# Moving the sums of adj's rows into layer 1, with three buffers for the logits and one for the rows

## The chip, the cores and the metric

The kernel runs on one core of a Trainium2 chip. The metric is the device time of one execution in microseconds (us): the median of the runs. Engines are called by the names of the profile: PE is TensorE, PEld its weight loads, DVE is VectorE, ACT is ScalarE, POOL is GpSimd, SP is SyncE. A "line" such as L551 is a line of the kernel that the profile belongs to; from layer 1 on, the changed kernel's line numbers are 3 to 8 higher than those of the kernel before (ahead of it one lower), and the experiments' are one or a few higher still.

## The reference

Four layers over a graph of N = 2708 nodes with 256 features. `adj` is a dense 2708 x 2708 matrix of non-negative weights, about 29 MB. Each layer is followed by a residual and a layernorm.

```python
x = layernorm(x + adj @ x * W0)                     # layer 0
x = layernorm(x + gat4(x, adj > 0, W1, a1))         # layer 1: four heads of attention, then layernorm
# layer 2, "edge" and "node" parts
dn  = diag(adj);  A = adj - diag(dn)
edge = gru(A @ x, x, edge_weights)
node = gru(mean over 3 heads of (softmax(logits where A != 0) * A) @ x @ Wk, x, node_weights)
x = layernorm(x + dn * edge + dn * node)
# layer 3
deg = adj.sum(axis=1) + 1
x = layernorm(x + concat(x, (adj @ (x @ Wn.T)) / deg) @ Wl.T)
```

Three things are needed of adj's rows: the diagonal, the places that are zero (`none`), and the sum of each row for layer 3 (`deg`). Layer 2 also needs, for each row and each of the three heads, the maximum of the logits and the sum of their exponentials; they are called the row statistics here. Names that the profile lines use: `z` holds the logits of one head for 128 rows, `arow` a tile of adj's rows, `tr` the transposes that TensorE makes of x, `xt` their copy by ScalarE (TensorE's next matmuls read it), `supt` ScalarE's copy of s, `sr` the transposed row statistics, `whh` and `wih` the weights of the gated unit. PSUM is the memory that TensorE accumulates in.

## The kernel before

The 22 row tiles of 128 rows are grouped in six spans (five of 512 columns, one of 148). The edge stage makes, for each span, `s = adj_t-block @ x` on TensorE, and the row statistics of its tiles on VectorE and ScalarE; the gated unit ("unit") of a span is emitted after the statistics of the next.

```python
early = [turn[:, i * CB * W : (i + 1) * CB * W]... for i in range(2)]   # two blocks in an idle buffer
...
def row_stats(t):                                   # edge stage
    a = load_rows(nc.gpsimd, rows, t, 2)            # two buffers for adj's rows
    z = rows.tile([P, N], F32, tag="z", bufs=2)
    nc.scalar.activation(z[:n], a[:n], AF.Identity, accum_out=degree[:n])   # the sum; z is not used
    nc.vector.tensor_scalar(degree[:n], degree[:n], 1.0, None, ALU.add)
    nc.vector.reciprocal(rdeg[:n, t : t + 1], degree[:n])
    ...                                             # diagonal
    nc.vector.tensor_scalar(none[:n], a[:n], 0.0, NEG_INF, ALU.is_equal, ALU.mult)
    for k in range(K):                              # K = 3 heads
        if k: z = rows.tile([P, N], F32, tag="z", bufs=2)
        nc.vector.tensor_tensor_reduce(out=z[:n], in0=e_b[:n, k, :], in1=none[:n], ..., accum_out=st[...])
        nc.scalar.activation(z[:n], z[:n], AF.Exp, scale=-1.0, bias=st[...], accum_out=den[:n])
        nc.vector.reciprocal(st[:n, t, 1, k : k + 1], den[:n])

for g, (lo, hi) in enumerate(spans):                # edge stage
    ...                                             # 22 x 2 matmuls s <- block, x
    for f in range(FC): nc.scalar.copy(supt[:, f, :w], acc[f][:, :w])
    for t in range(lo, hi): row_stats(t)
    if g == len(spans) - 1: store_stats(ps_e, rows, *spans[0])
    if last: edge(*last)                            # unit of the span before: 4 transposes, xt copies, 24 matmuls
    last = (g, supt)
edge(*last)
```

In layer 1, four heads are accumulated for each span, and each result is copied from PSUM by ScalarE (`sum`). The rest of layer 1 (normalisation with a power on GpSimd, transposes on TensorE, copies `xt` on ScalarE) follows a span later.

The softmax here doesn't subtract the row's maximum and nothing guards it: scores larger than these inputs give would overflow.

Of the kernel before, what the change touches and what calls it, by code (L numbers as in the profile page):

```python
# [8 lines left out]
F32 = mybir.dt.float32  # L9
# [4 lines left out]
AF = mybir.ActivationFunctionType  # L14
ALU = mybir.AluOpType
# [3 lines left out]
P = 128  # L19
# [7 lines left out]
def kernel(  # L27
# [37 lines left out]
    def sz(i):  # L65
        return min(P, N - i * P)
# [11 lines left out]
    def pool(name, bufs=1, **kw):  # L78
# [16 lines left out]

    turn = xpool.tile([P, NT * F], F32, name="turn")
    x0 = h3 = [turn[:, t * F : (t + 1) * F] for t in range(NT)]
    early = [
        turn[:, i * CB * W : (i + 1) * CB * W].rearrange("p (c w) -> p c w", w=W)
        for i in range(NT * F // (CB * W))  # L100
    ]

    fall_d = dram.tile([H, N], F32, name="fall_d")
    e_d = dram.tile([K, N], F32, name="e_d")
# [4 lines left out]
    u_parts = xpool.tile([P, NT, 3, K], BF16, name="u_parts")  # L109

    rdeg = xpool.tile([P, NT], F32, name="rdeg")
    diag = xpool.tile([P, NT], F32, name="diag")

    st = xpool.tile([P, NT, 2, K], F32, name="st")
# [38 lines left out]
    def load_rows(queue, pool, t, bufs):  # L153
        a = pool.tile([P, N], F32, tag="arow", name="arow", bufs=bufs)
        queue.dma_start(a[: sz(t)], adj[t * P : t * P + sz(t), :])
        return a
# [18 lines left out]
    def weights(pool, name, w):  # L175
        wt = pool.tile([P, w.shape[0] // P, w.shape[1]], F32, name=name)
        nc.sync.dma_start(wt, w.rearrange("(c p) j -> p c j", p=P))
        return wt
# [33 lines left out]
    with pool("l1keep") as keep:  # L212
# [56 lines left out]
        with (  # L269
# [63 lines left out]
            with pool("l1", 2) as l1:  # L333

                def layer1_rest(t, o):
                    n = sz(t)
                    layernorm(o, o, n)
                    nc.vector.tensor_tensor(o[:n], o[:n], gamma_b[:n], ALU.mult)
                    nc.vector.tensor_tensor(o[:n], o[:n], beta_b[:n], ALU.add)
                    nc.vector.tensor_tensor(o[:n], o[:n], xs[t][:n], ALU.add)  # L340
                    layernorm(xs[t], o, n)

                    xt = transposed(ps_t, l1, xs[t], n, "xt")
                    pm = ps_m.tile([P, 2 * F], F32, tag="pm", name="pm")
                    for f in range(FC):
                        nc.tensor.matmul(
                            pm[:n, :K], xt[:, f, :n], uw[:, f, :], start=(f == 0), stop=(f == FC - 1)
                        )
                    left = pm[:n, :K]
                    for i in range(3):  # L350
                        nc.vector.tensor_copy(u_parts[:n, t, i, :], left)
                        if i < 2:
                            r = small.tile([P, K], F32, tag="u_left", name="u_left")
                            nc.vector.tensor_tensor(r[:n], left, u_parts[:n, t, i, :], ALU.subtract)
                            left = r[:n]

                def layer1_end(lo, hi, sums):

                    for t in range(lo, hi):
                        n = sz(t)  # L360
                        at = (t - lo) * P
                        pt = ps_t.tile([P, 4, P], F32, tag="tr", name="tr")
                        for h in range(H):
                            nc.tensor.transpose(
                                pt[:n, h, : HD + 1], sums[h][: HD + 1, at : at + n], ident[: HD + 1, : HD + 1]
                            )
                        rden = small.tile([P, H], F32, tag="rdenh", name="rdenh")
                        nc.vector.reciprocal(rden[:n], pt[:n, :H, HD])
                        o = l1.tile([P, F], F32, tag="o", name="o")
                        nc.vector.tensor_tensor(  # L370
                            o[:n].rearrange("p (h d) -> p h d", d=HD),
                            pt[:n, :H, :HD],
                            rden[:n, :, None].to_broadcast([n, H, HD]),
                            ALU.mult,
                        )
                        layer1_rest(t, o)



                done = None  # L380
                for lo, hi in spans:
                    at, w = lo * P, width(lo, hi)
                    sums = []
                    for h in range(H):
                        acc = ps_acc.tile([P, 512], F32, tag="acc", name="acc")
                        for c in range(NT):
                            k = sz(c)
                            p = l1.tile([P, W], F32, tag="p", name="p", bufs=6)
                            nc.vector.scalar_tensor_tensor(  # L389
                                p[:k, :w], fall_b[:k, h, at : at + w], rise[:k, c, h : h + 1],  # L390
                                mask[:k, c, at : at + w], ALU.max, ALU.mult,
                            )
                            nc.tensor.matmul(  # L393
                                acc[: HD + 1, :w], hs[c][:k, h, :], p[:k, :w], start=(c == 0), stop=(c == NT - 1)
                            )
                        sb = l1.tile([HD + 1, W], F32, tag=f"sum{h}", name=f"sum{h}", bufs=1 + (h == 0))
                        nc.scalar.copy(sb[:, :w], acc[: HD + 1, :w])  # L397
                        sums.append(sb)
                        if h == 0 and done:
                            layer1_end(*done)  # L400

                    for t in range(lo, hi):
                        n = sz(t)
                        own = mask[:n, t, t * P : t * P + n]
                        nc.gpsimd.tensor_tensor(own, own, offdiag[:n, :n], ALU.mult, saturate=False)
                    done = (lo, hi, sums)
                layer1_end(*done)
# [106 lines left out]
    with (  # L514
# [3 lines left out]
        pool("ps_e", 2, space=PSUM) as ps_e,  # L518
        pool("ps_g", 4, space=PSUM) as ps_g,
    ):  # L520
        wih, whh = weights(ework, "wih", e_wih), weights(ework, "whh", e_whh)
        b = gru_columns(ework, e_bih, e_bhh)
        e_b = rows.tile([P, K, N], F32, name="e_b")
# [3 lines left out]

        def row_stats(t):
            n = sz(t)
            a = load_rows(nc.gpsimd, rows, t, 2)  # L530
            z = rows.tile([P, N], F32, tag="z", name="z", bufs=2)
            degree = small.tile([P, 1], F32, tag="degree", name="degree")
            nc.scalar.activation(z[:n], a[:n], AF.Identity, accum_out=degree[:n])  # L533
            nc.vector.tensor_scalar(degree[:n], degree[:n], 1.0, None, ALU.add)
            nc.vector.reciprocal(rdeg[:n, t : t + 1], degree[:n])
            blk = a[:n, t * P : t * P + n]
            dtmp = rows.tile([P, P], F32, tag="dtmp", name="dtmp")
            nc.vector.scalar_tensor_tensor(
                dtmp[:n, :n], blk, 1.0, ident[:n, :n], ALU.mult, ALU.mult, accum_out=diag[:n, t : t + 1]
            )  # L540
            nc.vector.tensor_tensor(blk, blk, offdiag[:n, :n], ALU.mult)
            none = rows.tile([P, N], BF16, tag="none", name="none", bufs=2)
            nc.vector.tensor_scalar(none[:n], a[:n], 0.0, NEG_INF, ALU.is_equal, ALU.mult)
            for k in range(K):
                if k:
                    z = rows.tile([P, N], F32, tag="z", name="z", bufs=2)

                nc.vector.tensor_tensor_reduce(  # L548
                    out=z[:n], in0=e_b[:n, k, :], in1=none[:n], scale=-1.0, scalar=HIGHEST,
                    op0=ALU.add, op1=ALU.min, accum_out=st[:n, t, 0, k : k + 1],  # L550
                )  # L551
                den = small.tile([P, 1], F32, tag="den", name="den")
                nc.scalar.activation(  # L553
                    z[:n], z[:n], AF.Exp, scale=-1.0, bias=st[:n, t, 0, k : k + 1], accum_out=den[:n]
                )
                nc.vector.reciprocal(st[:n, t, 1, k : k + 1], den[:n])
# [11 lines left out]
        for g, (lo, hi) in enumerate(spans):  # L568
            w = width(lo, hi)
            acc = [ps_s.tile([P, W], F32, tag=f"s{f}", name=f"s{f}") for f in range(FC)]  # L570
            for bi, (c0, c1) in enumerate(blocks):
                if loads % 5 < len(early):
                    s = load_block(early[loads % 5], lo, hi, bi, None)
                else:
                    s = load_block(ework, lo, hi, bi, 5 - len(early))
                loads += 1
                for c in range(c0, c1):
                    k = sz(c)
                    for f in range(FC):
                        nc.tensor.matmul(  # L580
                            acc[f][:, :w], xs[c][:k, f * P : (f + 1) * P], s[:k, c - c0, :w],
                            start=(c == 0), stop=(c == NT - 1),
                        )
# [365 lines left out]
```

## Time and profile before

| | us |
|---|---|
| Time, median of the runs (2274.83 to 2279.68) | 2276.75 |
| Layer 1, first matmul to the first matmul of the u sums | 457.6 |
| Edge stage, its first matmul to the node stage's first | 379.2 |
| of which: first pass to last exponential (statistics) | 329.3 |
| of which: last exponential to the node stage (tail) | 38.0 |
| Node stage and layer 3 | 1084.4 |

Two more answers on the whole edge stage are wanted for the comparison. The first is its row of the stretches' busy times (columns: stretch, its length, then busy us and number of instructions of PE, PEld, DVE, ACT, POOL; granted clock, DMA share, GB/s). The second is the list of what TensorE waited for there (total us, times, longest).

```profile
809.80:1189.00 379.20, 334.09 (x886) 156.72 (x886) 286.65 (x422) 267.37 (x267) 18.76 (x32) 0.94 0.57 174
```

```profile
PE tr L464 <- ACT xt L465: 24.1, 8, 15.5
PE tr L464 <- ACT sr L478: 8.6, 2, 6.7
PE s L580 <- DMA blk<-in_adj_t_dram: 3.2, 1, 3.2
...
PE gate L437 <- ACT xt L465: 2.5, 1, 2.5
```

TensorE, not VectorE, is the busiest engine of the stage: 334 of 379 us. It idles 379.2 - 334.1 = 45.1 us, and 24.1 + 2.5 = 26.6 us of this are waits for the xt copies that stand in ScalarE's queue.

### The profile page before, as it was taken

What the parts mean: (1) busy time and instruction counts of PE and PEld (TensorE: products, weight loads), DVE (VectorE), ACT (ScalarE), POOL (GpSimd) and SP (SyncE); (2) the same over time, 40 slices, a digit from 0 to 9 for tenths busy, and PEclk for the clock granted to TensorE, in tenths of its full rate; (3) what the DMA queues carried; (4) which work ended last, traced back from release to release, by engine and by line L of the source; (5) the groups of instructions that cost most, each with busy time, mean ns of one, the idle gap of its engine ahead of it and who ended that gap; (6) DMA issues with size and microseconds to landing.
All of it is one profiled execution on the core that took longest, in us unless ns stands there. A gap on an engine that the chain in (4) does not pass through costs nothing.

```text
span 2273.4 us, 19055 instructions
## 1 busy us (share of the span) xinstructions
PE 2141.9 (94%) x6729; PEld 1094.7 (48%) x6729; DVE 1404.6 (62%) x2747; ACT 601.9 (26%) x937; POOL 175.8 (8%) x258
## 2 busy tenths in 40 slices
PE   5999999999999899999669999999999999979998
PEld 4777733333334334444434444444444444658886
DVE  4555578999988547888846656646646646441111
ACT  0000000000000147877743333333333323320000
POOL 0111100101101110000000000000000000011111
PEclk9999999999999799999879999999999999989999
DMA  5343320000000187654153300301212000014443
GB/s 185 134 146 136 138 54 0 0 0 0 1 0 1 64 253 240 206 183 154 50 159 108 100 30 19 102 28 38 83 38 65 21 22 24 1 70 149 171 165 120
DMA packets 163910, 196.57 MB, mean 86 GB/s; under 512 B 17218, under 2 KB 145511, under 8 KB 155464
## 3 DMA queue, kind: packets, MB, share of 16 engines
q1 hardware_dynamic: 154204, 147.74, 20.8%
q0 software_dynamic: 9600, 47.51, 6.0%
q8 instruction: 55, 0.90, 0.2%
q14 instruction: 51, 0.42, 0.1%
HBM read 186.75 MB, written 8.46 MB: 86 GB/s over the span
## 4 chain that ended last, share of the span: by engine, by line
PE 72%; DVE 16%; ACT 3%; issue 3%; POOL 3%; DMA 2%; SPq 1%; POOLq 0%; ACTq 0%; DVEq 0%
PE acc L670 25%; PE acc L173 16%; PE acc L393 11%; PE gate L437 7%; DVE p L389 5%; PE s L580 4%; DVE z L548 3%; POOL bn_rs L128 2%; PE gate L629 2%; PE pz L187 2%; ACT z L553 1%; ACT z L533 1%; DVE bn_st L122 1%; PE u L493 1%; PE tr L135 1%
## 5 line engine op out<-in xcount | busy, mean ns | idle before, releaser
L670 PE MATMUL acc<-p,x 128*128 128x512 f32 (+2 forms) x1584 | 620.7, 546 | 2.0 <-DVE p L668 2.0
L173 PE MATMUL acc<-turn,strip 128*128 128x256 f32 (+2 forms) x1936 | 444.9, 385 | 0.5 <-ACT lwn L266 0.5
L393 PE MATMUL acc<-p,h 128*65 128x512 f32 (+3 forms) x1056 | 425.6, 552 | 6.5 <-DVE p L389 5.5
L670 PEld LDWEIGHTS acc<-p,x 128*128 128x128 f32 (+1 forms) x1584 | 280.7, 191 | 308.5 <-issue 263.0
L173 PEld LDWEIGHTS acc<-turn,strip 128*128 128x128 f32 (+2 forms) x1936 | 350.1, 186 | 86.5 <-issue 35.0
L389 DVE SCALAR_TENSOR_TENSOR p<-fall_b,rise,mask 128x512 f32<-128x512 f32 (+2 forms) x528 | 354.1, 682 | 25.6 <-PE acc L393 6.9
L668 DVE TENSOR_TENSOR p<-p,blk 128x512 f32<-128x512 f32 (+2 forms) x396 | 245.7, 626 | 193.4 <-ACT p L667 192.1
L667 ACT ACTIVATE p<-p 128x512 f32<-128x512 f32 (+2 forms) x396 | 225.7, 578 | 380.3 <-DVE p L664 378.5
L393 PEld LDWEIGHTS acc<-p,h 128*65 128x65 f32 (+1 forms) x1056 | 137.0, 140 | 262.7 <-issue 137.2
L548 DVE CUSTOM_DVE_ANT_0 z<-e_b,none 128x2708 f32<-128x2708 f32 (+1 forms) x66 | 195.3, 2966 | 6.2 <-DMA e_b<-e_d 5.7
L553 ACT ACTIVATE z<-z,st 128x2708 f32<-128x2708 f32 (+1 forms) x66 | 168.2, 2549 | 74.0 <-DVE st L548 74.0
L664 DVE TENSOR_SCALAR p<-st_b,e_col 128x512 f32<-128x512 f32 (+2 forms) x396 | 175.2, 447 | 11.6 <-PE acc L670 11.2
L128 POOL TENSOR_TENSOR bn_rs<-bn_ve,neg_half 128x1 f32<-128x1 f32 (+1 forms) x110 | 74.5, 677 | 1107.8 <-DVE bn_ve L126 1104.3
L137 ACT COPY xt<-tr 128x256 f32<-128x256 f32 x66 | 24.0, 364 | 473.1 <-PE tr L135 464.4
L580 PE MATMUL s<-blk,x 128*128 128x512 f32 (+2 forms) x312 | 124.9, 555 | 3.2 <-DMA blk<-in_adj_t_dram 3.2
L437 PE MATMUL gate<-xt,whh 128*128 128x512 f32 (+1 forms) x288 | 123.6, 552 | 4.2 <-ACT xt L465 2.8
L697 DVE SCALAR_TENSOR_TENSOR o<-acc,rdeg,o 128x256 f32<-128x256 f32 (+1 forms) x22 | 10.6, 483 | 164.9 <-PE acc L173 164.9
L580 PE MATMUL s<-turn,x 128*128 128x512 f32 (+3 forms) x216 | 86.7, 551 | 2.8 <-ACT supt L586 2.8
L580 PEld LDWEIGHTS s<-blk,x 128*128 128x128 f32 (+1 forms) x312 | 56.8, 193 | 67.4 <-issue 66.7
L437 PEld LDWEIGHTS gate<-xt,whh 128*128 128x128 f32 x288 | 53.1, 195 | 62.8 <-issue 51.7
L397 ACT COPY sum<-acc 65x512 f32<-65x512 f32 (+1 forms) x24 | 12.6, 531 | 228.8 <-PE acc L393 228.8
L449 DVE SCALAR_TENSOR_TENSOR g_r<-g_r,g_h 128x512 f32<-128x512 f32 (+1 forms) x24 | 15.0, 625 | 86.7 <-ACT g_h L442 86.7
(133 smaller groups left out, 1435.3 us busy)
## 6 DMA issues: line engine op xcount, KB each, us to landing
strip<-in_adj_t_dram SPq DMA_DIRECT2D x44, 1408.0 KB, 6.1
blk<-in_adj_t_dram SPq DMA_DIRECT2D x168, 256.0 KB, 4.7
arow<-in_adj_dram POOLq DMA_DIRECT2D x21, 1354.0 KB, 6.5
turn<-in_adj_t_dram SPq DMA_DIRECT2D x42, 256.0 KB, 5.3
st_b<-st_d SPq DMA_DIRECT2D x5, 1536.0 KB, 6.3
fall_b<-fall_d POOLq DMA_DIRECT2D x5, 1024.0 KB, 6.5
blk<-in_adj_t_dram SPq DMA_DIRECT2D x33, 128.0 KB, 2.7
e_b<-e_d POOLq DMA_DIRECT2D x5, 768.0 KB, 5.2
```

The source lines that it names most:

```text
L128: nc.gpsimd.tensor_tensor(rstd[:n], ve[:n], neg_half[:n], ALU.pow)
L173: nc.tensor.matmul(acc, s[:k, c, :n], rhs(c)[:k], start=(c == 0), stop=(c == NT - 1))
L389: nc.vector.scalar_tensor_tensor(p[:k, :w], fall_b[:k, h, at : at + w], rise[:k, c, h : h + 1], mask[:k, c, at : at + w], ALU.max, ALU.mult,)
L393: nc.tensor.matmul(acc[: HD + 1, :w], hs[c][:k, h, :], p[:k, :w], start=(c == 0), stop=(c == NT - 1))
L437: nc.tensor.matmul(g[:, :w], lt, rt, start=(q == 0), stop=(q == len(terms) - 1))
L548: nc.vector.tensor_tensor_reduce(out=z[:n], in0=e_b[:n, k, :], in1=none[:n], scale=-1.0, scalar=HIGHEST, op0=ALU.add, op1=ALU.min, accum_o ...
L553: nc.scalar.activation(z[:n], z[:n], AF.Exp, scale=-1.0, bias=st[:n, t, 0, k : k + 1], accum_out=den[:n])
L580: nc.tensor.matmul(acc[f][:, :w], xs[c][:k, f * P : (f + 1) * P], s[:k, c - c0, :w], start=(c == 0), stop=(c == NT - 1),)
L664: nc.vector.tensor_scalar(p[:q, :w], st_b[:q, k, :w], e_col[:q, c, k : k + 1], 0.0, ALU.add, ALU.min)
L667: nc.scalar.activation(p[:q, :w], p[:q, :w], AF.Exp)
L668: nc.vector.tensor_tensor(p[:q, :w], p[:q, :w], blks[bi][:q, c - c0, :w], ALU.mult)
L670: nc.tensor.matmul(acc[f][:, :w], xs[c][:q, f * P : (f + 1) * P], p[:q, :w], start=(c == 0), stop=(c == NT - 1),)
```

## The change

Its intent: the sum of a row (2.54 us on ScalarE for each of 22 tiles) is taken out of the edge stage, where ScalarE and VectorE wait for each other, into layer 1, where ScalarE is empty. adj's rows have to be read twice for it. The sum no longer takes a z buffer, a third z buffer is added, and the row buffer and one early block pay for the memory.

```diff
-    early = [turn[:, i * CB * W : ...] for i in range(...)]      # two blocks
+    early = turn[:, : CB * W]...                                 # one block
+    row = turn[:, CB * W : CB * W + N]
+    nc.gpsimd.memset(rdeg, 1.0)
 ... in layer 1
+    def row_degree(t):
+        nc.sync.dma_start(row[:n], adj[t * P : t * P + n, :])
+        degree = small.tile([P, 1], F32, tag="degree", name="degree")
+        nc.scalar.activation(row[:n], row[:n], AF.Identity, accum_out=degree[:n])
+        nc.gpsimd.tensor_scalar(rdeg[:n, t : t + 1], degree[:n], 1.0, None, ALU.add)
 ...
                         sums.append(sb)
                         if h == 0 and done:
                             layer1_end(*done)
+                        if lo + h < hi:
+                            row_degree(lo + h)
 ... in the edge stage
+    nc.vector.reciprocal(rdeg, rdeg)
 ...
-            a = load_rows(nc.gpsimd, rows, t, 2)
-            z = rows.tile([P, N], F32, tag="z", name="z", bufs=2)
-            degree = small.tile([P, 1], F32, tag="degree", name="degree")
-            nc.scalar.activation(z[:n], a[:n], AF.Identity, accum_out=degree[:n])
-            nc.vector.tensor_scalar(degree[:n], degree[:n], 1.0, None, ALU.add)
-            nc.vector.reciprocal(rdeg[:n, t : t + 1], degree[:n])
+            a = load_rows(nc.gpsimd, rows, t, 1)
 ...
-                if k:
-                    z = rows.tile([P, N], F32, tag="z", name="z", bufs=2)
+                z = rows.tile([P, N], F32, tag="z", name="z", bufs=3)
 ...
-                if loads % 5 < len(early): s = load_block(early[loads % 5], ...)
-                else:                      s = load_block(ework, ..., 5 - len(early))
+                if loads % 5 == 0: s = load_block(early, ...)
+                else:              s = load_block(ework, ..., 4)
```

More of the change, by code (lines that the diff above doesn't have):

```diff
@@ L97 @@
     x0 = h3 = [turn[:, t * F : (t + 1) * F] for t in range(NT)]
-    early = [
-        turn[:, i * CB * W : (i + 1) * CB * W].rearrange("p (c w) -> p c w", w=W)
-        for i in range(NT * F // (CB * W))
-    ]
+    early = turn[:, : CB * W].rearrange("p (c w) -> p c w", w=W)
+    row = turn[:, CB * W : CB * W + N]
     fall_d = dram.tile([H, N], F32, name="fall_d")
@@ L376, in layer1_end @@
                         layer1_rest(t, o)
+                def row_degree(t):
+                    n = sz(t)
+                    nc.sync.dma_start(row[:n], adj[t * P : t * P + n, :])
+                    degree = small.tile([P, 1], F32, tag="degree", name="degree")
+                    nc.scalar.activation(row[:n], row[:n], AF.Identity, accum_out=degree[:n])
+                    nc.gpsimd.tensor_scalar(rdeg[:n, t : t + 1], degree[:n], 1.0, None, ALU.add)
                 done = None
@@ L571 @@
             for bi, (c0, c1) in enumerate(blocks):
-                if loads % 5 < len(early):
-                    s = load_block(early[loads % 5], lo, hi, bi, None)
+                if loads % 5 == 0:
+                    s = load_block(early, lo, hi, bi, None)
                 else:
-                    s = load_block(ework, lo, hi, bi, 5 - len(early))
+                    s = load_block(ework, lo, hi, bi, 4)
                 loads += 1
```

## The prediction

> **What bounds the kernel now.** The busy time of each engine in six stretches comes first, because the share over the whole span mixes stages with different limits.
>
> ```profile
> core 0: us, PE busy (x) PEld busy (x) DVE busy (x) ACT busy (x) POOL busy (x), PEclk, DMA share, GB/s
> ...
> 304.00:761.00 457.00, 440.12 (x1259) 157.25 (x1259) 409.19 (x887) 19.40 (x44) 51.11 (x63) 0.99 0.01 1
> ...
> 831.60:1150.00 318.40, 291.71 (x744) 134.33 (x745) 264.03 (x372) 249.47 (x235) 14.10 (x24) 0.95 0.55 170
> 1150.00:1189.00 39.00, 25.51 (x98) 15.26 (x96) 13.69 (x32) 13.06 (x28) 2.25 (x4) 0.81 0.62 178
> 1189.00:2030.00 841.00, 828.36 (x2222) 385.25 (x2222) 486.82 (x1028) 282.91 (x515) 25.87 (x43) 1.00 0.17 52
> ```
>
> The reader is to see: layer 1 (304 to 761 us) is bound by TensorE and leaves ScalarE empty (19 of 457 us) and the DMA too (1 GB/s). The edge stage (810 to 1189 us, where the row statistics run) has VectorE at 264 and ScalarE at 249 of 318 us, and in its last 39 us nothing is full. The node stage after it is full of TensorE; the change doesn't touch it, nor layer 3.
>
> Then VectorE's groups in 821 to 1151 us, for what each tile of statistics waits for:
>
> ```profile
> L548 DVE CUSTOM_DVE_ANT_0 z<-e_b,none 128x2708 f32<-128x2708 f32 x63 | 186.5, 2967 | 6.1 <-DMA e_b<-e_d 5.7
> L543 DVE TENSOR_SCALAR none<-arow 128x2708 bf16<-128x2708 f32 x20 | 31.4, 1570 | 0.0
> L556 DVE RECIPROCAL st<-den 128x1 f32<-128x1 f32 x63 | 9.9, 157 | 17.6 <-ACT z L553 17.5
> ...
> L534 DVE TENSOR_SCALAR degree<-degree 128x1 f32<-128x1 f32 x20 | 3.0, 152 | 26.9 <-ACT z L533 26.8
> ```
>
> So VectorE stands still 26.9 us for the sums of adj's rows and 17.6 us for reciprocals behind ScalarE. In time order, one tile shows how the sum does it:
>
> ```profile
> 980.26 0.29 DVE L538 SCALAR_TENSOR_TENSOR dtmp<-arow,ident 128x128 f32<-128x128 f32 x1
> ...
> 983.11 0.16 DVE L556 RECIPROCAL st<-den 128x1 f32<-128x1 f32 x1 [2.48 <-ACT z L553]
> 985.56 0.15 DVE L534 TENSOR_SCALAR degree<-degree 128x1 f32<-128x1 f32 x1 [2.28 <-ACT z L533]
> ```
>
> The sum also takes one of the two z buffers for its unused output, so ScalarE can't start it early. Last, TensorE's timeline at the end of the stage:
>
> ```profile
> 1117.54 1.98 PE L437 MATMUL gate<-supt,wih 128*128 128x512 f32 x4
> 1134.99 0.69 PE L464 MATMUL tr<-ident,x 128*128 128x128 f32 x2 [15.47 <-ACT xt L465]
> 1140.23 1.12 PE L464 MATMUL tr<-ident,x 128*128 128x128 f32 x4 [4.55 <-ACT xt L465]
> 1141.38 3.11 PE L437 MATMUL gate<-xt,whh 128*128 128x512 f32 x4
> ```
>
> TensorE had finished its span matmuls and idled 20 us, because the little copies of xt stand in ScalarE's queue behind exps. The statistics end at 1151 us, gates run to 1174, and the node stage's first matmul is at 1189.
>
> **What the Trainium skill says.** "TensorE: Matmul & The Clock Gate", section on the array as 16 32×32 sub-arrays: ScalarE's and VectorE's queues are strict FIFO. The trace agrees: xt's copy at 1134.59 us came only after the exp of 1132.04. "ScalarE: Activation LUTs", Rules for kernel authors: about 0.3 us + 0.83 ns per element, for 2708 elements 2.55 us; the trace has 2.46 us plus an accumulator read of 0.19, overlapping to 2.54. "DMA: Bandwidth & Descriptors", Anatomy of one DMA: 2.0 us + bytes/436e3, for a 1354 KB row tile 5.2 us; the trace has a median of 6.5 (arow) and 6.1 (a strip of 1408 KB), which I use. "Perfetto Trace Analysis", Optimization Strategy: the same gap repeating can mean too few buffers; the gap of 2.28 us repeats in most tiles.
>
> **The change, part by part.**
>
> *1. Removed from the edge stage.* 22 sums on ScalarE of 2.54 us (56 us), 22 adds and 22 reciprocals of 0.15 us on VectorE, which cost 0.2 us a tile (4 us), and the wait of 26.9 us. With a third z buffer most of the 17.6 us should go too. VectorE's floor, from the spacing in the trace: 66 passes at 2.96 us = 196; 20 masks (none; two fall before) at 1.6 = 32; 19 diagonals at 0.45 = 8.5; three gated units' arithmetic, 30 x 0.62 = 18.6; diagonal blocks 4.5. Sum 260 us. I add 20 us for stalls that I expect to stay: 5 for blocks from DMA (4.8 now), 5 for ScalarE's small work in between, 5 for row loads, 5 for matching with TensorE. TensorE has its own floor of the same size: counting 0.858 us a matmul from its timeline, it ends span 4 near 1071 us, where VectorE without stalls gets at 1075. So 282 us with the last exp, against 329 now (822 to 1151).
>
> *2. One buffer for adj's rows.* A load can start when none has been read (0.55 us later in the trace) and takes 6.5 us, so 7 us; VectorE has three passes, 8.9 us, meanwhile. Hidden, unless a load is slow (the slowest took 9.8 us). In the start of the stage it costs a little: row tile 1 is now asked for after two e_b broadcasts and stands in VectorE's order between small copies on which TensorE's transposes wait. I put 2.5 us.
>
> *3. One early block, four in the other pool.* Five buffers as before. TensorE has one block (8 matmuls, 6.9 us) instead of two before it waits for loads, but does 5 gate matmuls there that come later otherwise. Zero net.
>
> *4. Added to layer 1.* 22 loads, sums and GpSimd adds. One buffer makes them a serial chain: 2.54 us sum + 0.2 to the issue + about 6 us for the load = 8.7 us each, an estimate from the durations above. The first load queues behind a 1 MB block, so I count from 302.5 us: sum k ends at 302.5 + 8.7k. In the built order ScalarE's queue has xt copies after sums 13, 15, 16 and 18, and GpSimd's has layernorm powers behind the adds 12, 13 and 15 to 17. Sum 15 ends at 433.0, while that xt copy ran at 426.6; sum 12 at 406.9 against a power at 405.5. TensorE waits in order for xt, so this is lost: 433.0 - 426.6 = 6.4 us. Each 0.5 us more per link adds some 7 us; at 8.2 us the loss is nothing. Some evictions of the accumulators get late too, but three accumulators hide that.
>
> *5. The end of the edge stage.* This is where the gain goes. In the built order the fourth unit's (span 3) elementwise work on VectorE comes after the last pass; in the kernel before, only spans 4 and 5 were left. Its gates fill the four PSUM buffers and TensorE stops. From the last exp on, in sequence: half of unit 3's gates, 12 matmuls x 0.858 + 0.7 = 11 us; the rest of span 5, 33 matmuls of 148 columns at 0.257 = 8.5; evictions and xt copies 3.3; unit 4's 24 matmuls 20.6; unit 5 as before (1163.2 to 1174.1) 10.9; then as before to the node stage 15. Sum 69 us, against 38 now (1151 to 1189).
>
> *Sum.* Layer 1 +6.4; start +2.5; statistics 282 - 329 = -47; tail 69 - 38 = +31. Together -7 us: 2275 - 7 = 2268. Since my 20 us of stalls is rather generous, I shade it to 2266.
>
> **The rivals.** *A: the whole wait comes back as time.* If the tail stayed at 38 us and layer 1 were free, 47 us would go, 2228. For it: the waits are real. Against it: the order of the queues is fixed, and it leaves three units behind the last pass. *B: layer 1's chain of loads is slower.* At 9.3 us a link, sum 15 ends at 442 and sum 18 at 469.9, 16 us after its xt copy is wanted: layer 1 loses 16 us and the time is about 2276. For it: a strip in layer 0 once took 7.1 us from issue to use. Against it: a broadcast ran beside that one. *C: TensorE and VectorE have nearly equal floors.* Each small delay then passes to the other; 15 us more of stalls gives 2281. *D: the row loads are exposed* with one buffer: 1 to 2 us in each of 20 tiles would give 2290. For it: DMA runs at 170 GB/s here and now more densely; against it: the median of 6.5 us.
>
> **Range and chances.** Without any stall in the statistics and none in layer 1 the same sums give about 2240, so a gain over 2% (below 2229.5) would need a shorter tail; a loss over 2% (above 2320.5) would need B and D together and more. Hence 2248 to 2284, and chances 0.04 faster, 0.94 same, 0.02 slower.
>
> **What would show it.** VectorE's wait for the sums is gone, and the spacing of the passes' tiles falls from 15 to about 12.7 us. Layer 1 grows from 457 to some 463 us, with TensorE waiting for xt's copies at about 425 to 440 us. The last exp ends near 1113 us and some 69 us pass from there to the first node matmul, near 1182. The prediction is wrong if the tail stays near 40 us (then A), if layer 1 grows by more than 12 us (B), or if VectorE waits on arow's DMA in most tiles (D).

The 2.55 us and 5.2 us that it takes from pages of the Trainium skill are estimates worked out from the pages' figures; its sums use the durations of the trace.

## The result, and the profile after

| | before | after | difference |
|---|---|---|---|
| Time, median of four runs | 2276.75 | 2255.27 (2250.58 to 2256.97) | -21.5 |
| Profiled run | 2273.4 | 2254.1 | -19.3 |
| Start of the edge stage | 809.8 | 810.4 | +0.6 |
| Edge stage's first matmul to first pass | 11.9 | 12.1 | +0.2 |
| Statistics, first pass to last exponential | 329.3 | 275.2 | -54.1 |
| Tail, last exponential to the node stage | 38.0 | 73.9 | +35.9 |
| Node stage and layer 3 | 1084.4 | 1082.5 | -1.9 |

The ratio of after to before is 0.9901, with a 95% interval of 0.9881 to 0.9921: "same" by the 2% rule, and a real gain of about 1%. A ratio is the mean time of one kernel's runs over that of the other's runs of the same rounds, so it is not quite the ratio of the medians quoted. The prediction said 2266, from 2275 and a sum of -7 us shaded to -9; the measured gain is 21.5 us, and the time lies inside the range of 2248 to 2284 that it gave.

The rows of the stretches after, in the same columns: layer 1, the whole edge stage, and in it the statistics and the tail.

```profile
305.70:764.90 459.20, 444.73 (x1261) 161.13 (x1262) 409.49 (x888) 74.11 (x88) 61.44 (x85) 0.97 0.17 62
810.40:1171.60 361.20, 331.91 (x886) 155.16 (x886) 281.15 (x378) 218.32 (x225) 19.72 (x33) 0.96 0.62 189
822.60:1097.70 275.10, 262.60 (x626) 116.29 (x627) 258.71 (x326) 196.01 (x179) 13.24 (x22) 0.98 0.68 208
1097.70:1171.60 73.90, 58.60 (x227) 34.40 (x225) 20.64 (x42) 20.77 (x43) 3.35 (x6) 0.91 0.37 107
```

Layer 1 now has ScalarE at 74 us instead of 19 and takes 459.2 us against 457.6; that 1.6 us is inside the scatter of the runs below (457.6 to 459.4 us over the kernel before, c_before and before_z3, which have no sums in layer 1; 458.3 for the mended changed kernel). In the edge stage TensorE does the same 886 matmul instructions in 332 us; what shrank is its idle time, from 45.1 to 361.2 - 331.9 = 29.3 us. What it waited for in the edge stage after:

```profile
PE tr L472 <- ACT sr L486: 7.8, 2, 7.4
PE s L583 <- ACT supt L589: 5.1, 2, 3.9
PE gate L445 <- DMA whh<-in_L_gnn_edge_Whh_dram: 5.0, 1, 5.0
PE gate L445 <- ACT xt L473: 3.5, 3, 2.5
PE tr L472 <- ACT xt L473: 2.1, 6, 0.5
```

The waits for xt fell from 26.6 to 3.5 + 2.1 = 5.6 us, that is by 21.0. A wait for the unit's weights of 5.0 us is new and one for a block of 3.2 us is gone; the wait for the evictions (supt) grew from 2.8 to 5.1. The net of all entries is the 16 us of idle time; the other 2 us of the stage's 18.0 are busy time (334.1 against 331.9 us). The granted clock of the stage was 0.96 instead of 0.94; that this made the 2 us was not tested.

VectorE's groups, for what a tile waits for:

```profile
L551 DVE CUSTOM_DVE_ANT_0 z<-e_b,none 128x2708 f32<-128x2708 f32 x63 | 186.5, 2967 | 6.2 <-DMA e_b<-e_d 5.9
...
L559 DVE RECIPROCAL st<-den 128x1 f32<-128x1 f32 x63 | 9.9, 157 | 4.3 <-ACT z L556 4.3
```

The passes are the same to a tenth of a us, the group of the sums (26.9 us of waits) is gone, and the reciprocals wait 4.3 us instead of 17.6. In time order, from the mask of one tile to that of the next:

```profile
1059.90 1.57 DVE L547 TENSOR_SCALAR none<-arow 128x2708 bf16<-128x2708 f32 x1
...
1073.75 1.56 DVE L547 TENSOR_SCALAR none<-arow 128x2708 bf16<-128x2708 f32 x1
```

This tile took 13.85 us, with five pieces of a unit's arithmetic of 0.69 us in it. TensorE at the end of the statistics, where the prediction expected it stopped for lack of PSUM buffers:

```profile
1092.46 1.98 PE L445 MATMUL gate<-xt,whh 128*128 128x512 f32 x4 [0.75 <-ACT xt L473]
...
1111.44 1.88 PE L445 MATMUL gate<-supt,wih 128*128 128x512 f32 x4
1113.16 6.96 PE L583 MATMUL s<-blk,x 128*128 128x148 f32 x54
```

TensorE goes through the fourth unit without a pause; it is simply late, and it is still at work long after VectorE is through. Last, ScalarE's queue in layer 1: the first sums, and the sum that the prediction was about.

```profile
304.50 2.46 ACT L381 ACTIVATE turn<-turn 128x2708 f32<-128x2708 f32 x1 [0.16 <-issue]
...
314.13 2.46 ACT L381 ACTIVATE turn<-turn 128x2708 f32<-128x2708 f32 x1 [7.08 <-DMA turn<-in_adj_dram]
...
426.14 2.46 ACT L381 ACTIVATE turn<-turn 128x2708 f32<-128x2708 f32 x1 [5.94 <-DMA turn<-in_adj_dram]
...
429.48 0.37 ACT L136 COPY xt<-tr 128x256 f32<-128x256 f32 x1 [0.78 <-PE tr L134]
```

The chain of loads is there. One link of it is a sum and the load of the next row into the same buffer; the 22 sums start from 304.5 to 488.4 us, (488.4 - 304.5) / 21 = 8.76 us a link. But the 15th sum begins at 426.14 and ends at 428.6, and the xt copy behind it waits for TensorE's transposes and not for the sum. The margin is 429.5 - 428.6 = 0.9 us.

### The profile page after: what moved, and what is told of

The parts are those of the page before. It is cut to its first block, busy times and chain, and to the rows that moved or that the text cites. A ratio compares the mean times of both kernels' runs of the same rounds, so it can differ in the third digit from the quotient of the medians.

```text
span 2254.1 us, 19100 instructions
## 1 busy us (share of the span) xinstructions
PE 2141.5 (95%) x6729; PEld 1096.7 (49%) x6729; DVE 1400.3 (62%) x2704; ACT 606.1 (27%) x937; POOL 185.2 (8%) x281
## 4 chain that ended last, share of the span: by engine, by line
PE 74%; DVE 16%; DMA 4%; POOL 3%; issue 2%; ACT 1%; SPq 1%; POOLq 0%; ACTq 0%; DVEq 0%
PE acc L673 25%; PE acc L172 16%; PE acc L399 11%; PE gate L445 8%; PE s L583 5%; DVE p L395 5%; DVE z L551 3%; PE gate L632 2%; POOL bn_rs L127 2%; PE pz L186 2%; DMA strip<-in_adj_t_dram 1%; DVE bn_st L121 1%; PE tr L134 1%; PE u L501 1%; PE pm L282 1%
## 5 line engine op out<-in xcount | busy, mean ns | idle before, releaser
L395 DVE SCALAR_TENSOR_TENSOR p<-fall_b,rise,mask 128x512 f32<-128x512 f32 (+2 forms) x528 | 354.1, 682 | 26.6 <-PE acc L399 8.0
L583 PE MATMUL s<-blk,x 128*128 128x512 f32 (+2 forms) x416 | 165.3, 554 | 4.0 <-ACT supt L589 3.9
L583 PEld LDWEIGHTS s<-blk,x 128*128 128x128 f32 (+1 forms) x416 | 75.5, 192 | 90.7 <-issue 85.3
L445 PEld LDWEIGHTS gate<-xt,whh 128*128 128x128 f32 x288 | 53.4, 196 | 69.7 <-issue 54.1
L381 ACT ACTIVATE turn<-turn 128x2708 f32<-128x2708 f32 (+1 forms) x22 | 54.1, 2461 | 89.1 <-DMA turn<-in_adj_dram 88.9
L315 DVE TENSOR_REDUCE low<-strip 128x1 f32<-128x2816 f32 x22 | 67.7, 3078 | 0.0
```

What stands on the lines that cost most here:

```text
L395: nc.vector.scalar_tensor_tensor(p[:k, :w], fall_b[:k, h, at : at + w], rise[:k, c, h : h + 1], mask[:k, c, at : at + w], ALU.max, ALU.mult,)
L445: nc.tensor.matmul(g[:, :w], lt, rt, start=(q == 0), stop=(q == len(terms) - 1))
L583: nc.tensor.matmul(acc[f][:, :w], xs[c][:k, f * P : (f + 1) * P], s[:k, c - c0, :w], start=(c == 0), stop=(c == NT - 1),)
```

## The experiments

Two theories lead through the runs; both came after the result. Theory F says that layer 1 gives the sums away for nothing, because the chain began some 4 us earlier than the prediction let it. Theory T says that TensorE bounds the edge stage, so that the gain is the part of its idle time that went, and shorter statistics alone give nothing. T's first half is partly bookkeeping: TensorE does the same work in both kernels, so a shorter stage must show as less idle time of TensorE. What has to be tested is which waits can go, and whether shorter statistics alone help. Rivals are named with each run. Every kernel has one mend, since the last row tile's narrow matmul in the u sums was not to be used in new kernels:

```diff
     u_parts = xpool.tile([P, NT, 3, K], BF16, name="u_parts")
+    nc.gpsimd.memset(u_parts, 0.0)
 ...
-                k = sz(c)                # u sums
+                k = P
```

Each run was timed in five rounds against the kernel before, on one chip for each group of four.

### Controls: c_before and c_after

The edit is the mend alone.

> The kernel before with one mend that every kernel of this study has: the last row tile's part of the u sums (20 rows of the mask) is multiplied with all 128 rows, the other 108 rows of u_parts being set to zero once. Nothing else differs. Both theories expect the time of the kernel before within 0.3%, a ratio of 0.997 to 1.003. Only if it lies outside do the other runs have to be read against it instead of against the kernel before.

> The changed kernel with the same mend. Expected: 0.990 of the kernel before (0.988 to 0.992), as the changed kernel itself. In its trace, layer 1 has no wait of TensorE for an xt copy, and TensorE's idle time between the first matmul of the edge stage and the first of the node stage is some 29 us, against 47 us in the kernel before.

Measured: 2275.33 us, ratio 0.9985 (0.9963 to 1.0007) for the mended kernel before; 2253.90 us, ratio 0.9897 (0.9877 to 0.9918) for the mended changed kernel. In the trace of the latter, TensorE waits for no xt copy in layer 1, and idles 360.3 - 333.9 = 26.4 us in the edge stage (29 expected; the 47 that the expectation gives for the kernel before is 45.1 by the rows above). The mend changes nothing that matters, and the result holds.

### no_sums: the changed kernel without the work in layer 1

```diff
-                        if lo + h < hi:
-                            row_degree(lo + h)
```

> The changed kernel without the row loads, the sums and the adds in layer 1 (wrong result on purpose: rdeg stays 1). Theory F (free): the chain of loads ran just ahead of the xt copies, its 15th sum ended at 428.6 us and the copy behind it was ready at 429.5, so nothing was lost in layer 1, and the 3.4 us by which layer 1 ended later came from layer 0's end (1.9 us) and a lower granted clock; then this run takes as long as the mended changed kernel within 2 us. Rival P (as predicted): layer 1 lost 6.4 us, which something else hid; then it is 6 us faster. Rival C: the 3.4 us are the sums' own price; then it is 3 to 4 us faster.

Measured: 2255.46 us, ratio 0.9898 (0.9876 to 0.9920), wrong result. Layer 1 took 458.2 us, against 458.3 in c_after. Moving 29 MB of loads and 56 us of ScalarE's work into layer 1 cost nothing that these rounds can see; rivals P and C fall.

### crowd: more traffic behind each row

```diff
                     nc.sync.dma_start(row[:n], adj[t * P : t * P + n, :])
+                    nc.sync.dma_start(turn[:n, : CB * W], adj[t * P : t * P + n, : CB * W])
```

> The changed kernel with a second load of 1 MB behind each row's load on the same queue, into a part of the buffer that is idle in layer 1 (result stays right). It makes each link of the chain longer than its 8.76 us; call the link L. Theory F with its margin of 0.9 us at the 15th sum: TensorE then waits for the xt copy behind the 15th sum, and layer 1 grows by 14 x (L - 8.76) - 0.9 us: with L = 9.3 by 7 us, with L = 10 by 16 us. If layer 1 grows by less than 2 us though L is above 9.3 us, the copies' place behind the sums doesn't matter and the whole mechanism of part 4 of the prediction is wrong.

Measured: 2254.67 us, ratio 0.9898 (0.9875 to 0.9920). A link stayed at (488.97 - 303.59) / 21 = 8.83 us, so the premise failed: the second load landed 7.9 us after its issue (median) against 5.8 us for the row's own, so during the sum of 2.54 us, and nothing was tested.

### late16, late64, late256: the chain made later

Single elements of a row, 16 (in late256: 8) apart, go first into the same buffer, so the first row must wait for them. The order of sums and xt copies in ScalarE's queue is unchanged.

```diff
+                    if t == 0:
+                        nc.sync.dma_start(row[:, 0 : 256 : 16], adj[:P, 0 : 256 : 16])     # late16; 64, 256 elements likewise
                     nc.sync.dma_start(row[:n], adj[t * P : t * P + n, :])
```

> The load of the crowd run turned out to lie wholly in the pauses of the chain (a link stayed 8.8 us), so that run tested nothing. Here the whole chain is made later: a load of 128 x 16 single elements goes ahead of the first row's load into the same buffer; the order of ScalarE's queue is the same as in the changed kernel. Call d the time by which the second sum starts later after layer 1's first matmul than in the changed kernel (8.4 us). Theory F with the margin of 0.9 us at the 15th sum: layer 1, from its first matmul to the first u matmul (458.3 to 459.3 us in the changed kernel and its mended copy), grows by d - 0.9, and TensorE waits for the xt copy at some 430 us. With d below 0.9 nothing. Rival N: the copies' place behind the sums never mattered; layer 1 stays the same whatever d is.

> The same with 128 x 64 single elements, four times as many, so that d is larger; it must be above 0.9 us for a test. Theory F: layer 1 grows by d - 0.9. Rival N: not at all. If F holds in both runs, part 4 of the prediction had the mechanism right and failed only in the time at which it let the chain begin (302.5 us, against 298.2 counted back from the trace: first sum's end 306.96 less one link of 8.76).

> 128 x 16 elements moved the chain by 0.2 us and 128 x 64 by 3.2 us, of which the faster links after it gave back all but about 0.1 us by the 15th sum (its end, 428.27 us, was just the moment at which its xt copy was wanted), so neither went clearly past the margin. Here 128 x 256 elements, an estimate of 12 to 16 us from these two. The order of sums and xt copies in ScalarE's queue is that of the changed kernel up to the copies in question. Theory F: the end of the 15th sum comes later than its xt copy's input by some 10 to 14 us, TensorE waits that long for it, layer 1 grows from 458 to 459 by this amount to 468 to 473 us, and the time is 2263 to 2268 us, a ratio near 0.995. Rival N: layer 1 stays at 458 to 459 us and the ratio at 0.990.

Measured, with the time from layer 1's first matmul to the second sum (8.4 us in the changed kernel) for d:

| run | d, us | layer 1, us | median, us | ratio |
|---|---|---|---|---|
| c_after | 0.1 | 458.3 | 2253.90 | 0.9897 |
| late16 | 0.3 | 457.2 | 2252.28 | 0.9914 |
| late64 | 3.3 | 459.1 | 2253.94 | 0.9915 |
| late256 | 18.6 | 473.1 | 2270.04 | 0.9975 |

The two small delays stayed inside the margin: that of late16 is below 0.9 us, and in late64 the links up to the 15th sum were shorter (8.4 us) and gave the delay back. They decide nothing, since a chain that is late and not late enough looks the same under both theories. late256 went past it. Its stretch from the first matmul of layer 1 to the u sums, then ScalarE at the 15th sum, then GpSimd at the add of the 12th, which comes earlier in the same chain:

```profile
306.40:779.40 473.00, 446.73 (x1260) 160.03 (x1260) 409.88 (x888) 74.84 (x88) 61.44 (x85) 0.97 0.22 63
```

```profile
443.73 2.46 ACT L382 ACTIVATE turn<-turn 128x2708 f32<-128x2708 f32 x1 [6.10 <-DMA turn<-in_adj_dram]
...
446.19 0.35 ACT L137 COPY xt<-tr 128x256 f32<-128x256 f32 x1
```

```profile
420.69 0.21 POOL L383 TENSOR_SCALAR rdeg<-degree 128x1 f32<-128x1 f32 x1 [8.18 <-ACT turn L382]
420.86 0.57 POOL L128 TENSOR_TENSOR bn_rs<-bn_ve,neg_half 128x1 f32<-128x1 f32 x1
```

The xt copy now starts the moment the 15th sum is read out (446.19), and the layernorm's power (bn_rs) the moment the 12th sum's add is done (420.86); VectorE waited 11.8 us for that power, and TensorE then for VectorE. Layer 1 grew by 473.1 - 458.3 = 14.8 us (d less 0.9 us would be 17.7; the links after it were shorter again, 8.5 us). Rival N falls. Theory F expected 468 to 473 us for layer 1 and "near 0.995" for the ratio: layer 1 came out at the upper end, and the ratio 0.0025 higher. The wait did not show as TensorE waiting for xt, as F had it, but one step earlier, through GpSimd. So the mechanism of part 4 of the prediction is real, on both queues it named; in the changed kernel it just does not reach the copies.

A 0.35 us copy and a 0.57 us power each stood behind an instruction that waited for a load: the strict order of the queues, which the prediction took from the Trainium skill for ScalarE and VectorE, is seen here on GpSimd too.

### two_passes: less work for VectorE and ScalarE

```diff
-            for k in range(K):
+            for k in range(K - 1):       # in row_stats
```

> The changed kernel with two of the three passes for each row tile (wrong result on purpose). It takes 22 x 2.97 = 65 us of work off VectorE and 22 x 2.55 = 56 us off ScalarE in the edge stage. Theory T: after the change TensorE bounds this stage (332 us busy of 361 before the first matmul of the node stage; 29 us idle, of which 13 to 14 at its end), so only its waits for ScalarE (some 7 us) and part of the end can go: 5 to 15 us faster than the changed kernel. Rival V: the statistics still set the end, as the prediction's sum is built: 45 to 65 us faster.

Measured: 2265.16 us, ratio 0.9969 (0.9949 to 0.9989), wrong result. This is some 10 us slower than the changed kernel; theory T had expected 5 to 15 us less, rival V 45 to 65 less, so both forecasts missed. The stage as a whole, its tail, and TensorE's longest wait in it:

```profile
811.10:1184.90 373.80, 336.29 (x886) 156.83 (x886) 218.57 (x312) 162.06 (x181) 20.47 (x33) 0.94 0.60 183
...
1038.90:1184.90 146.00, 129.97 (x412) 68.12 (x412) 28.96 (x58) 31.01 (x62) 3.88 (x7) 0.93 0.26 74
```

```profile
PE s L584 <- ACT supt L590: 12.4, 4, 5.8
```

The statistics ended at 1038.9 us, 59 us earlier than in the changed kernel, and the node stage began 13 us later. The tail doubled to 146 us, of which TensorE is busy 130. So rival V falls outright: the end of the statistics does not set the end of the stage. TensorE's idle time grew to 373.8 - 336.3 = 37.5 us; the evictions of its accumulators (supt) alone hold it 12.4 us instead of 5.1, and its busy time is 336.3 instead of 331.9. Fewer passes also change when everything in the queues gets its turn, and why the result is worse was not pursued. So the run shows that shorter statistics don't shorten the stage from here on; it doesn't show that nothing but TensorE could.

### sums_only: the sums moved, all buffers as before

```diff
-            a = load_rows(nc.gpsimd, rows, t, 1)
+            a = load_rows(nc.gpsimd, rows, t, 2)
-                z = rows.tile([P, N], F32, tag="z", name="z", bufs=3)
+                z = rows.tile([P, N], F32, tag="z", name="z", bufs=2)
 # and two early blocks; row lies over the second
```

> The sums moved into layer 1, but two z buffers, two buffers for adj's rows and two early blocks as in the kernel before. Theory T: what matters is that VectorE's 27 us of waits for the sums go; with TensorE as the bound the 17 us for the reciprocals don't count, so nearly the whole gain comes: 0.989 to 0.992 of the kernel before. Rival Z: the third z buffer makes half the gain: 0.994 to 0.997.

Measured: 2251.05 us, ratio 0.9908 (0.9889 to 0.9926). Within the noise the whole gain comes without the third z buffer, and the single row buffer costs nothing either. TensorE idles 358.1 - 330.3 = 27.8 us. Rival Z falls. Not separated by any run is whether the gain comes by the 56 us taken off ScalarE's queue or by VectorE's waits for the sums, which go at the same time; both can let the xt copies come earlier.

### before_z3: the third z buffer, nothing moved

```diff
 # kernel before
-    a = load_rows(nc.gpsimd, rows, t, 2)
+    a = load_rows(nc.gpsimd, rows, t, 1)
-    z = rows.tile([P, N], F32, tag="z", name="z", bufs=2)      # both places
+    z = rows.tile([P, N], F32, tag="z", name="z", bufs=3)
```

> The kernel before, sums still in the edge stage, with three z buffers and one buffer for adj's rows in place of two and two. Theory S: the gain of the change comes from taking the sums' 56 us off ScalarE, whose queue holds the xt copies and evictions that TensorE waits for; then a third buffer gives little: 0.996 to 1.002, with TensorE still idle for 40 us or more in the edge stage. Rival Z: a third buffer lets ScalarE start a sum before VectorE needs it, so that the wait of 27 us goes without moving anything: 0.990 to 0.993.

Measured: 2269.35 us, ratio 0.9968 (0.9951 to 0.9984). TensorE idles 373.9 - 338.5 = 35.4 us, under the 40 that theory S expected, and its waits for xt are:

```profile
PE tr L465 <- ACT xt L466: 10.5, 4, 9.1
...
PE gate L438 <- ACT xt L466: 4.8, 2, 2.5
```

These 15.3 us lie between the 26.6 of the kernel before and the 5.6 of the changed one. VectorE still waits 22.4 us for the sums. So the buffer by itself is worth about a third of the gain, and perhaps nothing: its interval reaches from a sixth to a half, and that of the mend alone (c_before, 0.9963 to 1.0007) overlaps it. With the sums gone it is worth nothing that these rounds can see.

### sr_slots and slots_xt: towards less idle time at the end

sr_slots removes the longest wait left. A second buffer for sr found no room (no run shows it), so the second copy goes to other partitions of the same buffer:

```diff
-        sr = pool.tile([2 * K, W], F32, tag="sr", name="sr")
+        sr = pool.tile([P, W], F32, tag="sr", name="sr") if slot < 2 else srs[0]
+        srs[:] = [sr]
+        sr = sr[slot % 2 * 32 : slot % 2 * 32 + 2 * K]
 ...
-                        store_stats(ps_n, nwork, *spans[g + 1])
+                        store_stats(ps_n, nwork, *spans[g + 1], slot=g + 1)
```

> The changed kernel with two places for the transposed statistics (sr) where it has one in the node stage. In the changed kernel TensorE stands 7.4 us before the node stage's first matmul, since the second copy into sr waits until the first store has left it. Theory T (TensorE's idle time is what the time consists of here): 6 to 7.5 us faster than the changed kernel, a ratio of 0.9865 to 0.9875. Rival: another wait of the same length is behind it (the broadcast of the statistics): less than 2 us, 0.989 to 0.990.

Measured: 2253.78 us, ratio 0.9900 (0.9884 to 0.9916), no gain where theory T expected 6 to 7.5 us; the rival was right, with another wait than the one it named. What ScalarE waited for at the node stage's start:

```profile
ACT xt L474 <- DMA edget<-yt: 5.9, 1, 5.9
```

The node stage's xt lies in memory of the edge stage's yt, and the copy must wait until the last unit's store has read it.

slots_xt has the two places as well, two z buffers, and makes the last unit's xt ahead of the fourth's gates:

```diff
                 store_stats(ps_e, rows, *spans[0])
+                last_xt = rows_t(ps_e, ework, lo, hi, 2)      # two xt buffers
 ...
-        edge(*last)
+        edge(*last, last_xt)
```

> A version meant to beat both: the changed kernel with two z buffers (the run sums_only says that the third is worth nothing), the two places for sr, and the last unit's xt made before the unit ahead of it, with a second xt buffer from the room that z leaves; that takes away TensorE's wait of 2.5 us before the last unit. Theory T: 8 to 10 us faster than the changed kernel, 0.985 to 0.987. Rival: two z buffers with one buffer for adj's rows are worse than either alone: 0.989 or more.

Measured: 2245.85 us (2244.70 to 2247.73, four runs), ratio 0.9871 (0.9850 to 0.9892), correct; near the lower end of what theory T expected, 8 to 10 us under the changed kernel.

```profile
807.90:1159.50 351.60, 333.13 (x887) 155.52 (x887) 281.01 (x378) 218.85 (x225) 19.91 (x33) 0.96 0.63 192
```

TensorE's idle time is 351.6 - 333.1 = 18.5 us. In the same rounds this is 7.9 us under sr_slots, with ranges that do not touch, so it beats the kernel before. The changed kernel was not in these rounds; its slowest and fastest runs elsewhere (2250.58 to 2257.86 us) lie above it too. How much of the 7.9 us belongs to the earlier xt and how much to the new places in memory, which also took the wait for yt away, was not separated.

## Why the prediction was right or wrong

The direction was right. The size was not: a sum of -7 us against -19.3 in the profiled runs.

**Layer 1, +6.4 us: the largest net miss.** The step that failed is "The first load queues behind a 1 MB block, so I count from 302.5 us: sum k ends at 302.5 + 8.7k." The link was right (8.7 predicted, 8.76 measured). The beginning was not: the block's loads were issued from 290.2 us, the first row's load at 297.0, and the first sum was over at 306.96, so the count starts at 306.96 - 8.76 = 298.2. Those 4.3 us are most of it; layer 1 itself also ran some 2 to 3 us later than in the trace of before, which moved the xt copies away from the sums. The chain then passes the copies with 0.9 us to spare. no_sums shows that the loss is zero, and late256 that the mechanism is there once the chain is late. The edge stage began +0.6 us later in the end, which is the measured value of this term; over the runs here without a delayed chain that start scatters from 807.0 to 812.0 us.

**Start of the edge stage, +2.5 us.** Measured +0.2. The early TensorE wait did move, from a block (3.2 us) to the unit's weights (5.0), but the first pass waits for the broadcast of e_b in both kernels (5.7 and 5.9 us).

**Statistics, -47 us, and tail, +31 us.** Both mechanisms were there: the wait for the sums is gone, the floor of VectorE was well worked out (260 against a busy time of 258.7 in the statistics), and the tail grew by about as much as predicted. Two sizes were off. The step "I add 20 us for stalls that I expect to stay" was too generous: all reciprocals 6.7, blocks 4.5 and rows 2.5 make 13.7 us, and the statistics shrank by 54.1. In the tail, "half of unit 3's gates, 12 matmuls x 0.858 + 0.7 = 11" was too small: at the last exponential (1097.7) TensorE was only some 5 us into its fourth unit and took until 1113.2 for it, 15.5 us, not stopped by PSUM but late. The tail grew by 35.9. The other parts of the tail fitted within 1 us.

These two misses belong together. In the kernel before, the last statistics held TensorE: the lines of the prediction show it waiting 15.47 and 4.55 us for xt copies behind exps. In the changed kernel the statistics are through while TensorE is still in its fourth unit, so what they gain beyond that point, the tail loses again. In two_passes they ended 59 us earlier still, and the stage did not get shorter. This is theory T in the main; two of its four forecasts of size failed (two_passes, sr_slots), so it doesn't say how much idle time a given edit frees. Read by TensorE, the stage lost 18.0 us, where the prediction's three terms for it make -47 + 31 + 2.5 = -13.5. The prediction's view of the stage as "VectorE first, then the tail" came near only because it had counted TensorE's remaining matmuls in the tail.

**Node stage and layer 3, nothing.** Measured -1.9. The change does not touch them; over all fourteen traces here this stretch varies between 1082.3 and 1084.4 us, so it is within the scatter.

In sum the miss of 12.2 us is 5.8 in layer 1, 2.3 at the start, 7.1 in the statistics less 4.9 back in the tail, and 1.9 of scatter. The shading to 2266 made up for 2 of them.

**The rivals.** A (the whole wait comes back) fell: the tail is 73.9 us. It could not come true while TensorE does the same matmuls, since it had only 45 us of idle time to give. B (a slower chain) fell by the link of 8.76 us. C (equal floors, small delays passed on) was nearest to theory T in thought, but put the loss where there was none. D (exposed row loads) fell: VectorE waited for rows 2.5 us in all, and sums_only, with two row buffers, is no faster.

## What to carry to other kernels

Before a wait on one engine is counted as gain, look for the engine with the most busy time in that stage and, for a change that takes no work off that engine, take its idle time as the most that can be gained; here 45 us, of which 16 went. Work moved under another stage cost nothing here, and the condition is that the queues it joins reach the next instruction that somebody waits for in time. So put the two moments side by side and state the margin: 0.9 us held, and a delay of 18.6 us cost 14.8. When a change has several parts, try each alone; here the move alone gave all of the gain, and the buffers none.

## What the Trainium skill lacked or had wrong

- "Perfetto Trace Analysis", section "Optimization Strategy", says that a gap repeating on the engine that should be saturated can mean too few buffers; the prediction left out the condition on the engine. VectorE's repeating gaps here (26.9 us for the sums, 17.6 us for reciprocals) looked like this, but a third buffer with the sums moved gained nothing (0.9908 with two, 0.9897 with three, intervals overlapping). The page has a rule for which engine to look at, the highest occupancy; in the edge stage that is TensorE (334.1 of 379.2 us, VectorE 286.7). What it lacks is how much such gaps on another engine are worth: of the 44.5 us on VectorE all but 4.3 went, and the stage lost 18.0.
- "DMA: Bandwidth & Descriptors", section "Measured (HBM→SBUF, 128 partitions, SWDGE, issued from GpSimd)", gives about 10.5 ns a packet, from a 64-packet transfer, and doesn't say whether this is for one DMA engine or for all of them together. Here, for loads from SP's queue, 24,576 more single elements from late64 to late256 took 18.6 - 3.3 = 15.3 us more: 0.62 ns each over all, or 10 ns each on one engine if they are spread evenly over the 16.
- No page that was used says how long a serial chain of load, sum and next load through one buffer is: 8.76 us for 1354 KB here, of which the sum is 2.54.
